# A two-layer block on one Trainium2 core: mean correlation with q and k exchanged, bias columns loaded by DMA, and the order of small work in the front and of the third batch changed

## The chip, the cores and the metric

The kernel runs on one core of a Trainium2 chip. The metric is device time in microseconds (us) of one execution. Five engines run in parallel, each in the order of its own instruction stream: TensorE (PE; its weight loads are shown apart as PEld), VectorE (DVE), ScalarE (ACT), GpSimd (POOL) and SyncE (SP). SP, ACT and POOL also issue DMAs, each into a queue of its own.

## What is computed

The input is x, 8 batches of 256 tokens of 256 features, and a context ctx of the same shape. Four residual steps follow each other, each on the layer norm of x:

```python
x = x + L0_xattn(layernorm(x), ctx, ctx, Wq, bq, Wout, bout)
x = x + L0_ffn(layernorm(x), centroids, ln_g, ln_b, w1, b1, w2, b2)
x = x + L1_xattn(layernorm(x), ctx, Wq, bq, Wkv, bkv, Wp, bp)
x = x + L1_ffn(layernorm(x), gate_W, w1_e, w3_e, w2_e, w1_s, w3_s, w2_s)

# L0_xattn: q, k, v have 16 features; corr is over the 256 positions
q, k, v = [(t @ Wq + bq).transpose(0, 2, 1) for t in (Q, K, V)]
corr = real(ifft(fft(q) * conj(fft(k)))).mean(axis=(0, 1))
W, I = top_k(corr, 12); W = softmax(W)
R = sum(w * roll(v, -shift) for w, shift in zip(W, I))
return tile_over_16_heads(R).reshape(8, 256, 256) @ Wout + bout

# L0_ffn: balanced assignment. Expert e takes the 256 tokens with the
# highest score for its centroid among those not yet taken, in turn.
h = layernorm(routed) ; h = gelu(h @ w1[e] + b1[e]) @ w2[e] + b2[e]

# L1_xattn: ordinary attention of 16 heads of 16, keys and values from ctx
# L1_ffn: top 2 of 8 experts (silu(x w1) * (x w3)) w2, plus 8 shared ones
```

## The kernel before

The 2,048 tokens lie in 16 tiles of 128 partitions (X for x, C for ctx; XT and CT are their transposes). The tile framework's scheduler is off: every engine runs its instructions in the order of the program text, so a wait of one instruction holds all that stand behind it on that engine. The one thing taken out of line is a queue, `work`, of products in steps of about 0.43 us: first the products of the second layer's keys and values, later those of the first layer's experts. `fill(us)` takes steps from it until so much time is used, and stands wherever PE would wait for another engine.

The stages, with the lines that matter here:

- **Loads (L1306 to L1342).** x and ctx come in eight loads on SP, the weights and biases behind them; bq, WZ and the centroids on ACT's queue. Two bias rows (`bq1`, `brow`) lie on one partition and are turned into columns on PE by `column` (L1256, products with `one1`).
- **Constants (L1493 to L1533).** On POOL and DVE: ident, `flip` (ones on the anti-diagonal, L1512), `a16` (L1507), the clearing of VA (L1523), `bsel`.
- **First projections.** `turn` transposes x and ctx; `stats_x` with its `newton()` gives each token's factor of the layer norm; `project` (L1447) makes q and k in one PSUM tile (`pqk`), batches stacked over the partitions. The factors, expanded (`rexp`, L1589) and transposed (`pR`, L1614), scale q; the bias is added to k (L1625).
- **Correlation (L1680 to L1777).** `pg` is the 256x256 product of k with q. Written to DRAM twice side by side (`Gd`) and read back with rows one element longer, its diagonals become columns (`DG`), and a product with a constant averages them: `pcorr`. While DG is on its way, PE transposes k (`vT`), multiplies Wout by flip (`woutr`, L1719; `wrt`, L1740), transposes boutb (`bt`), makes the first score product (`psx`) and takes `fill(1.73)`.
- **Shifts (L1780 to L1949).** The top 12 are found on DVE, their softmax weights written to DRAM (`Wd`) and read back skewed as a circulant (`CW`). `pr3` is CW times vT, `R3` its scaled copy, `pp` the product with woutr, `PB` that with boutb added. Meanwhile PE makes `ps0`, the row groups (`copy_rows`, two products of 128x512 each that put X into PSUM, where PB is added later), and small products for the scores (`pw`, L1887). `stay_warm` (L1929) puts a product that nobody reads behind pr3 and pp.
- **Scores and search.** X is completed, its scores for the centroids are made, and from L2202 a threshold search on DVE and PE finds each expert's tokens in turn, while PE runs the experts already found and the queue's products. `attention_columns` (L1369) is a generator of small preparations for the second attention, moved on by `next(columns)` at fixed places.
- **Second attention (L2960 to L3075).** A loop over batches and two halves of heads. Each turn makes `scores` (PE, L2687), exponentials (ACT, L2695) and the `values` of the turn before (PE, L2702). Batch b + 2 is prepared meanwhile: `add_y` adds the expert layer's rows (loaded two batches ahead by `load_y`), `batch_stats` makes mean and factor on DVE and POOL, `norm_q` normalises on DVE (L2616), `turn_q` transposes (L2640), `queries` projects (L2654); `add_bias` adds a bias to X on POOL (L2632). For the third batch (number 2) these lines stand in the turns of batch 0.
- **Second experts.** From here to the end PE runs the shared and the routed experts.

Of the kernel before, what the change touches and what calls it, by code (L numbers as in the profile page):

```python
# [9 lines left out]
F32 = mybir.dt.float32  # L10
# [4 lines left out]
ALU = mybir.AluOpType  # L15
# [1071 lines left out]
def fast_path(  # L1087
# [87 lines left out]
    one1 = const.tile([1, 1], F32, name="one1")  # L1175
    nc.vector.memset(one1, 1.0)
# [79 lines left out]
    def column(pool, tag, row, n):  # L1256

        pcol = pool.tile([P, n], F32, tag=tag, name="pcol")
        for j in range(n):
            nc.tensor.matmul(  # L1260
                pcol[:, j : j + 1],
                row[:, j * P : (j + 1) * P],
                one1,
                start=True,
                stop=True,
            )
        return pcol

# [26 lines left out]
    bq1 = pa.tile([1, DH], F32, name="bq1")  # L1295
    wout = pa.tile([P, KC, D], F32, name="wout")
    boutb = pa.tile([P, D], F32, name="boutb")
# [5 lines left out]
    brow = pst.tile([1, 2, H, DH], F32, name="brow")  # L1303
# [16 lines left out]
    nc.scalar.dma_start(out=bq1, in_=L0_xattn_bq.unsqueeze(0))  # L1320
# [6 lines left out]
    nc.scalar.dma_start(out=cen[:, 2, :], in_=L0_ffn_ln_b.partition_broadcast(E))  # L1327
    for src, dst in (
        (L0_xattn_Wout.rearrange("(lc p) n -> p lc n", p=P), wout),
        (L1_xattn_bq.unsqueeze(0), brow[:, 0].rearrange("o h d -> o (h d)")),  # L1330
        (bkv[:, 0, :].unsqueeze(0), brow[:, 1]),
        (L1_xattn_Wkv.rearrange("(kc p) n -> p kc n", p=P), wkv_in),
        (L1_xattn_Wq.rearrange("(kc p) n -> p kc n", p=P), wq),
        (L0_xattn_bout.partition_broadcast(P), boutb),
        (L0_ffn_ln_g.rearrange("(kc p) -> p kc", p=P), gbc[:, 0, :]),
        (L0_ffn_ln_b.rearrange("(kc p) -> p kc", p=P), gbc[:, 1, :]),
        (L0_ffn_b1.rearrange("e (fc p) -> (e fc) p", p=P), b1r),
    ):
        nc.sync.dma_start(out=dst, in_=src)
# [21 lines left out]
    bcol = pk.tile([P, 2, NB], F32, name="bcol")  # L1361
# [7 lines left out]
    def attention_columns():  # L1369


        pc = column(ps_k, "pm", brow.rearrange("o a h d -> o (a h d)"), 2 * NB)
        yield
        nc.vector.tensor_copy(bcol.rearrange("p a c -> p (a c)"), pc)
# [10 lines left out]
        pn = ps_k.tile([P, NB], F32, tag="pm", name="pn")  # L1385
        for c in range(NB):
            for kc in range(KC):
# [6 lines left out]
                )  # L1394
        nc.scalar.activation(qmax, pn, AF.Copy, scale=257.0)
# [51 lines left out]
    def project(which, weights, src):  # L1447

        for m in range(2):
            for kc in range(KC):  # L1450
                for g in range(4):
# [8 lines left out]
                    )  # L1460

# [9 lines left out]
    def rstd(mvs, r1, scale, eps, eng, mr=None):  # L1471
# [31 lines left out]
    a8 = pa.tile([P, 8], F32, name="a8")  # L1503
    nc.vector.tensor_reduce(
        a8, ident.rearrange("p (a i) -> p a i", i=16), AX.X, ALU.add
    )
    a16 = pa.tile([P, NCT, 16], F32, name="a16")  # L1507
    nc.vector.memset(a16, 0.0)
    for r in range(NCT):
        nc.vector.tensor_copy(a16[:, r, 8 * r : 8 * r + 8], a8)  # L1510

    flip = pa.tile([P, P], F32, name="flip")  # L1512
    nc.gpsimd.memset(flip, 1.0)
    nc.gpsimd.affine_select(
        out=flip,
        in_=flip,
        pattern=[[1, P]],
        compare_op=ALU.is_equal,
        fill=0.0,
        base=1 - P,  # L1520
        channel_multiplier=1,
    )
    nc.gpsimd.memset(VA[:, :, :, DH:], 0.0)  # L1523
    nc.gpsimd.memset(VA[:, :, :, DH : DH + 1], 1.0)
    bq8 = pa.tile([1, B, DH], F32, name="bq8")
    nc.gpsimd.tensor_copy(bq8, bq1.unsqueeze(1).to_broadcast([1, B, DH]))
# [9 lines left out]
    bqc = pa.tile([P, 1], F32, name="bqc")  # L1536
# [47 lines left out]
    newton = stats_x(12, nc.gpsimd)  # L1584
    turn(X, XT, 12, act, act)
    newton()

# [7 lines left out]
    turn(C, CT, 8, act, dve)  # L1595
    project(0, WC, XT)
    turn(C, CT, 12, act, dve)
    pc = column(ps_k, "pm", bq8.rearrange("o b c -> o (b c)"), 1)
    nc.vector.tensor_copy(bqc, pc)

# [10 lines left out]
    project(1, WZ, CT)  # L1611
# [11 lines left out]
    columns = attention_columns()  # L1623
    next(columns)
    nc.vector.tensor_scalar(qk[:, 1, :], pqk[:, 1, :], bqc, None, ALU.add)  # L1625
# [49 lines left out]
    )  # L1675
    cc.close()

# [6 lines left out]
    for tt in range(2):  # L1684
        nc.tensor.matmul(
            pgs[tt],
            qk[:, 1, tt * P : (tt + 1) * P],
            qk[:, 0, :],
            start=True,
            stop=True,  # L1690
        )
# [4 lines left out]
    for r in range(2):  # L1696
# [10 lines left out]
        in_=Gd[0, :].rearrange("(tt p w) -> p tt w", p=P, w=W2 + 1)[:, :, 0:S],  # L1707
    )

# [6 lines left out]

    pw = ps_t.tile([P, KC, D], F32, tag="pt", name="pw")
    for lc in range(KC):
        nc.tensor.matmul(  # L1719
            pw[:, lc, :], flip, wout[:, KC - 1 - lc, :], start=True, stop=True  # L1720
        )
    woutr = pa.tile([P, KC, D], F32, name="woutr")
    nc.scalar.copy(woutr, pw)
# [7 lines left out]
    for kc in range(KC):  # L1731
        pc = ps_t.tile([P, E], F32, tag="pt", name="pc")
        nc.tensor.transpose(pc, cg[:, kc * P : (kc + 1) * P], ident[:E, :E])
        nc.vector.tensor_copy(cenP[:, kc, 0:E], pc)
# [3 lines left out]
    for dc in range(KC):  # L1738
        for lc in range(KC):
            nc.tensor.matmul(  # L1740
                pw[:, dc, lc * P : (lc + 1) * P],
                wout[:, KC - 1 - lc, dc * P : (dc + 1) * P],
                flip,
                start=True,
                stop=True,
# [1744 lines left out]
```

## Time and profile before

| what | us |
|---|---|
| runs: lowest, median, highest of 3 | 883.21, 883.58, 884.36 |
| profiled execution, its own time | 878.96 |
| its span (first to last instruction) | 877.3 |
| PE busy in the span | 857.4 |
| DVE, ACT, POOL busy | 309.2, 265.6, 211.1 |
| mean granted PE clock | 0.997 of full |

The profile is of one execution, whose time is a little under those of the runs; differences within it are read against its own span. A matmul's row gives its start and its modelled duration; rows of one kind that follow each other are joined, with their number behind an x. In square brackets stands how long the engine had been idle before the row and what ended that.

### The profile page before, as it was taken

The numbers are of one execution on the slowest core, as the hardware profiler recorded it, in microseconds if no ns is written. First come the engines' busy times: TensorE is split into PE (matmuls) and PEld (weight loads), VectorE is DVE, ScalarE is ACT, GpSimd is POOL, SyncE is SP. The second block draws the span as 40 slices with busy tenths as digits, with TensorE's granted clock in tenths as the row PEclk, the third lists the DMA queues.
The fourth block names the chain that finished last, engine by engine and source line by source line (L and its number), as shares of the span: only waits on it lengthen the run. The fifth ranks groups of instructions, "written<-read, shape, count | busy, mean of one in ns | idle before, by whom it ended". The sixth has DMA issues, their size and how long they took to land. (4 is left out here: it accounts for less than half of the span.)

```text
span 877.3 us, 11190 instructions
## 1 busy us (share of the span) xinstructions
PE 857.4 (98%) x4204; PEld 535.2 (61%) x4204; DVE 309.2 (35%) x1028; ACT 265.6 (30%) x495; POOL 211.1 (24%) x292
## 2 busy tenths in 40 slices
PE   8899999999799999999999999999999999999997
PEld 7547788788355555545668474747464656474746
DVE  7388876502556665561111112021111111111011
ACT  4255543423677675321110111111111111111110
POOL 7061213311236364423310020111111121111200
PEclk9999999999999999999999999999999999999999
DMA  7485469731600001361110645564646434311130
GB/s 250 161 222 174 142 212 302 251 120 55 168 13 26 1 20 38 112 238 44 68 50 30 188 131 159 160 176 156 181 151 178 155 93 113 86 13 12 15 107 27
DMA packets 86282, 105.21 MB, mean 120 GB/s; under 512 B 7979, under 2 KB 76812, under 8 KB 86188
## 3 DMA queue, kind: packets, MB, share of 16 engines
q1 hardware_dynamic: 77706, 91.10, 32.6%
q0 software_dynamic: 7920, 13.02, 7.0%
q8 instruction: 35, 0.57, 0.3%
q10 hardware_dynamic: 594, 0.30, 0.1%
q14 instruction: 27, 0.22, 0.1%
HBM read 80.60 MB, written 25.37 MB: 121 GB/s over the span
## 5 line engine op out<-in xcount | busy, mean ns | idle before, releaser
L3119 DVE TENSOR_TENSOR A<-A,pu 128x512 f32<-128x512 f32 x96 | 66.0, 687 | 365.1 <-PE pu L3110 358.4
L3118 ACT ACTIVATE A<-pgt 128x512 f32<-128x512 f32 x96 | 57.4, 598 | 271.4 <-PE pgt L3110 271.3
L3179 POOL DMA_INDIRECT Od<-Y,ids x32 | 49.4, 1545 | 307.1 <-ACT Y L3192 215.0
L3110 PE MATMUL pgt<-RT,wa 128*128 128x512 f32 x256 | 121.1, 595 | 0.0
L3110 PE MATMUL pu<-RT,wb 128*128 128x512 f32 x256 | 120.3, 592 | 0.0
L3132 PE MATMUL py<-wc,A 128*128 128x256 f32 x512 | 111.8, 379 | 0.0
L3132 PEld LDWEIGHTS py<-wc,A 128*128 128x128 f32 x512 | 96.7, 190 | 13.3 <-issue 0.5
L2695 ACT ACTIVATE ex<-p,scale 128x512 f32<-128x512 f32 x128 | 77.2, 690 | 31.9 <-PE p L2687 30.7
L3110 PEld LDWEIGHTS pu<-RT,wb 128*128 128x128 f32 x256 | 48.6, 190 | 61.2 <-issue 60.0
L3110 PEld LDWEIGHTS pgt<-RT,wa 128*128 128x128 f32 x256 | 47.6, 190 | 54.9 <-issue 54.5
L2408 PE MATMUL ph<-RT,w 128*128 128x256 f32 x256 | 61.4, 389 | 0.2 <-ACT A L2417 0.2
L2425 PE MATMUL py<-w,A 128*128 128x256 f32 x256 | 61.3, 388 | 0.0
L2425 PEld LDWEIGHTS py<-w,A 128*128 128x128 f32 x256 | 46.6, 190 | 6.5
L2408 PEld LDWEIGHTS ph<-RT,w 128*128 128x128 f32 x256 | 45.3, 190 | 8.4 <-ACT A L2417 1.1
L2417 ACT ACTIVATE A<-ph,b1c 128x256 f32<-128x256 f32 x64 | 29.9, 472 | 58.4 <-PE ph L2408 56.5
L2927 POOL DMA_INDIRECT Td<-HP,to x32 | 31.6, 988 | 62.6 <-DMA Td<-HP,to 59.6
L3110 PE MATMUL pgt<-HT,wa_-1_2742 128*128 128x512 f32 x96 | 45.5, 596 | 0.0
L3110 PE MATMUL pu<-HT,wb_-1_2743 128*128 128x512 f32 x96 | 45.1, 592 | 0.0
L3192 ACT ACTIVATE Y<-py,R 128x256 f32<-128x256 f32 x32 | 15.1, 473 | 96.6 <-PE py L3132 93.5
L2687 PE MATMUL p<-QM,KT 32*128 32x512 f32 x256 | 42.9, 650 | 0.4 <-DVE QM L2668 0.4
L3132 PE MATMUL py<-wc_-1_2744,A 128*128 128x256 f32 x192 | 41.9, 379 | 0.0
L3132 PEld LDWEIGHTS py<-wc_-1_2744,A 128*128 128x128 f32 x192 | 36.4, 190 | 5.8 <-issue 1.0
(467 smaller groups left out, 991.6 us busy)
## 6 DMA issues: line engine op xcount, KB each, us to landing
w<-in_L_ffn_w_dram SPq DMA_DIRECT2D x16, 1024.0 KB
wa<-in_L_ffn_w_e_dram SPq DMA_DIRECT2D x8, 1024.0 KB
wb<-in_L_ffn_w_e_dram SPq DMA_DIRECT2D x8, 1024.0 KB
wc<-in_L_ffn_w_e_dram SPq DMA_DIRECT2D x8, 1024.0 KB
R<-Td SPq DMA_DIRECT2D x8, 530.0 KB
sa<-in_L_ffn_w_e_dram SPq DMA_DIRECT2D x16, 256.0 KB
sb<-in_L_ffn_w_e_dram SPq DMA_DIRECT2D x16, 256.0 KB
sc<-in_L_ffn_w_e_dram SPq DMA_DIRECT2D x16, 256.0 KB
```

The lines of the kernel that those rows point to most:

```text
L2408: nc.tensor.matmul(ph, w1[:, kc, f * P : (f + 1) * P], RT[:, kc, :], start=(kc == 0), stop=(kc == KC - 1),)
L2417: nc.scalar.activation(A[:, f, :], ph, AF.Gelu_apprx_tanh, bias=b1c[:, e, f : f + 1])
L2425: nc.tensor.matmul(py, A[:, f, r * P : (r + 1) * P], w2[:, f, :], start=(f == 0), stop=(f == NF - 1),)
L2687: nc.tensor.matmul(ps[g].rearrange("p m q -> p (m q)"), KT[rows, c, k0 : k0 + P], QM[b][rows, c].rearrange("p m q -> p (m q)"), start=True ...
L2695: nc.scalar.activation(e4[:, g], ps[g], AF.Exp, scale=scale)
L2927: nc.gpsimd.indirect_dma_start(out=Td, out_offset=bass.IndirectOffsetOnAxis(ap=to[g][:, k, j : j + 1], axis=0), in_=HP[:, GT * g + j, :], ...
L3110: nc.tensor.matmul(ps, w_[:, kc, fs], xs[kc], start=(kc == 0), stop=(kc == KC - 1),)
L3118: nc.scalar.activation(a, pgt, AF.Silu)
L3119: nc.vector.tensor_tensor(a, a, pu, ALU.mult)
L3132: nc.tensor.matmul(py, A[:, f, s : s + P], wc[:, f, :], start=(f == 0), stop=(f == NF - 1))
L3179: nc.gpsimd.indirect_dma_start(out=Od, out_offset=bass.IndirectOffsetOnAxis(ap=ids, axis=0), in_=Y, in_offset=None, compute_op=ALU.add,)
L3192: nc.scalar.activation(Y, py, AF.Copy, scale=R[:, i, D + e : D + e + 1])
```

## The change

- q and k change places in `pg`: the columns of the product are those of k. The diagonals run the other way, so DG is read from offset 1, CW with rows one element shorter, and vT's halves are taken in reverse. With that `flip`, `woutr` and the products with flip go; `wrt` is made by transposes, and `pp` uses Wout itself.
- The bias columns come by DMA: `bqc` through a copy of bq in DRAM (`bqd`, ACT's queue), `bcol` from L1_xattn_bq and through `bkd` (SP), `boc` from bout. `column`, `one1`, `bq1`, `bq8`, `brow` and `bt` go.
- `project` runs over kc outside and m inside and yields after each kc; `pR` stands between the halves of the second call. k's bias is added on ACT. The last `newton` is called with DVE.
- `rowsel` is made on POOL from a constant; the centroids' transposes stand before `pg`; b1's transpose and the parts of `attention_columns` stand elsewhere.
- `fill(1.73)` becomes `fill(4.3)`.
- After the top 12, three row groups instead of five stand before `pr3`; the other two stand where `stay_warm` stood.
- In the second attention `add_y(2)` and `batch_stats(2)` follow `norm_q(1)`, and `norm_q(2)` follows `turn_q(1)`.

```diff
-    nc.scalar.dma_start(out=bq1, in_=L0_xattn_bq.unsqueeze(0))
+    nc.scalar.dma_start(
+        out=bqd.rearrange("o (b c) -> (o b) c", b=B),
+        in_=L0_xattn_bq.partition_broadcast(B),
+    )
...
+    nc.scalar.dma_start(out=bqc, in_=bqd.rearrange("o (p x) -> p (o x)", x=1))
     for src, dst in (
+        (bkv[:, 0, :].unsqueeze(0), bkd.rearrange("o (h d) -> o h d", h=H)),
         (L0_xattn_Wout.rearrange("(lc p) n -> p lc n", p=P), wout),
-        (L1_xattn_bq.unsqueeze(0), brow[:, 0].rearrange("o h d -> o (h d)")),
-        (bkv[:, 0, :].unsqueeze(0), brow[:, 1]),
+        (L1_xattn_bq.rearrange("(c p) -> p c", p=P), bcol[:, 0, :]),
         (L1_xattn_Wkv.rearrange("(kc p) n -> p kc n", p=P), wkv_in),
         (L1_xattn_Wq.rearrange("(kc p) n -> p kc n", p=P), wq),
+        (bkd.rearrange("o (c p) -> p (o c)", p=P), bcol[:, 1, :]),
         (L0_xattn_bout.partition_broadcast(P), boutb),
+        (L0_xattn_bout.rearrange("(kc p) -> p kc", p=P), boc),
...
-        for m in range(2):
-            for kc in range(KC):
+        for kc in range(KC):
+            for m in range(2):
...
+            yield
...
-    newton = stats_x(12, nc.gpsimd)
+    newton_l = stats_x(12, nc.gpsimd)
     turn(X, XT, 12, act, act)
     newton()
+    turn(C, CT, 8, act, dve)
+    newton_l(nc.vector)
...
-    project(1, WZ, CT)
+    projected = project(1, WZ, CT)
+    next(projected)
     pR = ps_a.tile([P, S], F32, tag="pg", name="pR")
...
-    columns = attention_columns()
-    next(columns)
-    nc.vector.tensor_scalar(qk[:, 1, :], pqk[:, 1, :], bqc, None, ALU.add)
+    list(projected)
+    nc.scalar.activation(qk[:, 1, :], pqk[:, 1, :], AF.Identity, bias=bqc)
...
-            qk[:, 1, tt * P : (tt + 1) * P],
-            qk[:, 0, :],
+            qk[:, 0, tt * P : (tt + 1) * P],
+            qk[:, 1, :],
...
-        in_=Gd[0, :].rearrange("(tt p w) -> p tt w", p=P, w=W2 + 1)[:, :, 0:S],
+        in_=Gd[0, :].rearrange("(tt p w) -> p tt w", p=P, w=W2 + 1)[:, :, 1 : S + 1],
...
+    columns = attention_columns()
     next(columns)
-    fill(1.73)
+    pb1 = ps_t.tile([P, E * NF], F32, tag="pt", name="pb1")
+    nc.tensor.transpose(pb1, b1r, ident[: E * NF, : E * NF])
+    b1c = pr.tile([P, E, NF], F32, name="b1c")
+    nc.scalar.copy(b1c.rearrange("p e f -> p (e f)"), pb1)
+    fill(4.3)
...
-        in_=bass.AP(wd.tensor, wd.offset + 1, [[WD + 1, P], [P, 2], [1, S]]),
+        in_=bass.AP(wd.tensor, wd.offset + P - 1, [[WD - 1, P], [P, 2], [1, S]]),
...
-    for b in order_b[:3]:
-        copy_rows(b, ps_t, "pt")
...
-    pw = ps_a.tile([P, 4, 32], F32, tag="pg", name="pw")
+    pw = ps_t.tile([P, 4, 32], F32, tag="pt", name="pw")
...
-        if j == 0:
-            copy_rows(order_b[3], ps_t, "pt")
-        elif j == 1:
-            copy_rows(order_b[4], ps_k, "pm")
+    copy_rows(order_b[0], ps_t, "pt")
+    copy_rows(order_b[1], ps_t, "pt")
+    small_products(0)
+    small_products(1)
+    copy_rows(order_b[2], ps_t, "pt")
+    small_products(2)
...
-                vT[:, sc, :],
+                vT[:, 1 - sc, :],
...
-    stay_warm(pr3[:, 2:4, :].rearrange("p a q -> p (a q)"), 1)
+    copy_rows(order_b[3], ps_t, "pt")
...
-    stay_warm(pp2[:, 1, :], 1)
+    copy_rows(order_b[4], ps_k, "pm")
...
     norm_q(1, nc.vector, nc.vector)
+    add_y(2)
+    batch_stats(2, "q")
     add_bias(0)
...
                 turn_q(1)
+                norm_q(2, nc.vector, nc.vector)
                 queries(1, 0)
                 queries(1, 1)
-                add_y(2)
-                batch_stats(2, "q")
...
                 else:
-                    norm_q(2, nc.vector, nc.vector)
                     add_bias(2)
```

## The prediction

> **What bounds the kernel now.** I read the page's totals first, then a table of windows, then the order in time of the windows in which TensorE (PE) is not full.
>
> ```profile
> span 877.3 us, 11190 instructions
> ...
> PE 857.4 (98%) x4204; PEld 535.2 (61%) x4204; DVE 309.2 (35%) x1028; ACT 265.6 (30%) x495; POOL 211.1 (24%) x292
> ```
>
> PE is idle for 877.3 - 857.4 = 19.9 us in all. More than that can be gained only by taking PE work away or by clock. The table says where the idle time is (window, its length, PE's busy time first; the column after POOL is the granted clock):
>
> ```profile
> 0.00:20.00 20.00, 17.24 (x159) 14.29 (x160) 15.90 (x62) 8.61 (x15) 15.27 (x39) 1.00 0.84 274
> 20.00:31.00 11.00, 9.77 (x61) 6.78 (x62) 4.19 (x16) 3.14 (x7) 3.59 (x15) 1.00 0.23 73
> 40.00:57.00 17.00, 14.47 (x99) 6.80 (x98) 11.71 (x51) 7.38 (x20) 6.96 (x19) 1.00 1.09 325
> 79.00:100.00 21.00, 21.00 (x140) 16.22 (x139) 18.70 (x89) 11.27 (x25) 2.90 (x3) 1.00 0.35 119
> 230.00:240.00 10.00, 6.07 (x48) 3.12 (x52) 5.24 (x13) 3.88 (x8) 2.76 (x6) 0.98 1.08 291
> 240.00:260.00 20.00, 20.00 (x171) 10.20 (x165) 9.72 (x25) 14.54 (x25) 4.18 (x14) 0.92 0.05 15
> ```
>
> So there are three places: the front up to 57, bound by chains of dependent steps; the search beside the experts from 79, where PE is full and each product removed counts; and 230 to 240, with 3.93 us idle and a lower clock behind it. The front's rows (start, duration, engine, line, in brackets the wait):
>
> ```profile
> 19.06 0.49 POOL L1589 COPY rexp<-R 128x256 f32<-128x256 f32 x1
> ...
> 20.48 1.05 PE L1260 MATMUL pcol<-one,brow 1*128 1x1 f32 x8
> ...
> 21.47 1.13 PE L1685 MATMUL pg<-qk 128*128 128x256 f32 x4
> ...
> 30.28 1.13 PE L1777 MATMUL pcorr<-DG,mean_w 128*128 128x256 f32 x4 [1.03 <-DMA DG<-Gd]
> ...
> 39.80 1.13 PE L1933 MATMUL pr<-vT,CW 128*128 128x128 f32 x8 [0.47 <-PE pw L1898]
> ...
> 41.40 0.48 DVE L1942 TENSOR_SCALAR R<-pr,rtot 128x256 f32<-128x256 f32 x1 [0.66 <-PE pr L1929]
> ...
> 43.54 0.42 DVE L1949 TENSOR_TENSOR PB<-pp,boutb 128x256 f32<-128x256 f32 x1 [1.66 <-PE pp L1929]
> ```
>
> R3 and PB wait on L1929, the two dummy products, not on the products they read. The attention's rows:
>
> ```profile
> 224.51 1.23 DVE L2607 TENSOR_TENSOR b_t<-b_r,b_ve 128x2 f32<-128x2 f32 x1 [0.81 <-POOL b_r L2602]
> ...
> 237.99 0.78 PE L2640 MATMUL pt<-ident,h 128*128 128x128 f32 x4 [3.60 <-DVE h L2616]
> ...
> 239.81 1.94 PE L2702 MATMUL pv<-ex,VA 128*32 128x256 f32 x16
> 239.87 2.42 ACT L2695 ACTIVATE ex<-p,scale 128x512 f32<-128x512 f32 x4 [4.05 <-PE p L2687]
> ...
> 241.67 2.15 PE L2687 MATMUL p<-QM,KT 32*128 32x512 f32 x8
> ```
>
> PE waits 3.60 us for batch 2's normalised rows, and then the same products take twice as long (1.94 against 1.07 at 243.75; 2.15 against 1.17): a window of 3.4 us at half clock, 1.7 us lost.
>
> **Part 1, third batch sooner.** Before, add_y(2) starts on DVE at 233.41, POOL's Newton steps end at 237.40, norm_q(2) runs 237.43 to 238.16. Now add_y(2) and its statistics follow norm_q(1), which ends at 227.10, or 225.9 since the 1.23 us row loses its cover (POOL's bias add, 224.46 to 225.72, now comes later). Add 0.68 + 1.2 + 0.2: about 228.0. POOL takes 2.1 (235.34 to 237.40 before): 230.2. norm_q(2) follows turn_q(1)'s copy at 230.27 and ends near 231.0. PE needs it at 234.39, where pv of 233.32 ends, so the wait goes. What is late next is ACT: its exponentials run 2.42 per half, back to back from 233.41: 235.83, 238.25. Then the last pv of the pair starts near 238.5 and queries(2) near 239.6, against 244.75: **-5.1**. Bounds: -3.6 (the wait alone, the clock window falling elsewhere) and -5.6 (all idle 3.9 plus 1.7). Behind it the attention is PE-bound (20.00 of 20), so the gain stays. Moved with it: the VA copies at 227.02 come 1 to 1.5 later on DVE, before their readers; POOL's two bias adds run 230.3 to 232.9, read much later; load_y(4) stands on SP ahead of the weights issued from 226.74 and costs these under 1 us, hundreds before use; yg(2), issued from 214.5, is there.
>
> The row of 224.51 shows a DVE instruction that takes 1.23 instead of 0.16 (its twin at 215.53) until POOL's add ends. [...]
>
> **Part 2, front up to pcorr.** The flips (L1719 1.03, ACT 0.59), boutb's transposes (0.38) and brow's columns (1.05) leave PE; all but the last lay in the wait for DG. The first chain is rexp -> pR -> Rq -> qk -> pg. Chunk 8's Newton is still called twice on POOL (its name is rebound only for the last chunk), so rexp keeps its 19.06; VA's 3.50 us memset is now ahead of ident's select, which shifts the start of DVE's statistics by some 0.2. pR now stands between the halves of project(1): pR 19.75 to 20.45, second half 1.15 more, ACT's qk copy 0.5, so pg at 22.2 against 21.47: **+0.7** for pg, G and pcorr (31.0). Bounds 0 (rexp early enough) to +1.0 (ident's delay in full). In the wait for DG stand now 10 key products for 4 (fill 4.3 for 1.73): PE is ready at about 30.5, ahead of 31.0, so they are covered; were G early they would cost the difference.
>
> Bias columns: on SP one load of 1 KB to DRAM and three of 4-byte pieces replace brow's two. The trace's two loads of that kind (gbc) issue at 13.57 and 15.08, b1r at 15.85; at 1.5 each b1r moves to about 18, landing near 21. First readers now: bqm and pb1, ahead of the keys, about 26. Gd's issue stands behind them on SP, at 23.75. Covered by 5 us: 0. On ACT's queue a wait for bqd stands ahead of the table load (2.94); the first copy is at 5.98, the load and warm end 1.5 after start: 0, bound +0.5.
>
> **Part 3, pcorr to the search.** Before: pr3 starts 9.5 after pcorr since PE does five row groups (1.12 each) and pw's bank must be read first. Now only three groups and pw in another bank come before it, so PE is free 7.0 after pcorr, and pr3 waits for CW, whose last packets come 8.2 after pcorr (38.48), with 0.25 to its release: 8.45. That is -1.05. Without L1929 R3 and PB start at their products' ends: 41.40 -> 40.95 and 43.54 -> 43.1, in all -0.83; the two row groups fill the holes instead. With +0.7: -1.15 at the search (56.93). It meets a second bound: the first expert's rows go through DMA queues that the 40:57 row shows full (325 GB/s), and what is issued behind CW comes 0.25 earlier at most. I take **-0.9** for front and start, bounds -1.9 and +0.7. The small moves at 55.95 to 57.5 (pn, b1c, rowsel) sit beside DVE's chain: 0.
>
> **Part 4, products moved out of the full stretch.** Six products of two matmuls, 0.216 from start to start (95.75: six in 1.46), are 2.6 us. In the orders of both kernels two to three of the six are missing where the queue of work has run empty, near 97 to 102 and 156.5, and there PE waits for DVE's or POOL's result anyway (0.44 at 156.56). So three to four count: **-1.4**, bounds 0 and -2.6.
>
> **Sum**: -5.1 - 0.9 - 1.4 = -7.4. The profiled run took 878.96 (span 877.3): 871.6. The runs' median is 883.58, 4.62 above it; by the same difference the forecast is **876.2**. The ends of all terms give -2.9 and -10.1: 880.7 and 873.5.
>
> **Rivals.**
> - Everything counts (all six products, the front uncapped): -10.1, 873.5. For: PE is at 21.00 of 21. Against: the empty queue and the full DMA. 0.15.
> - The front nets a loss and the products move nothing: -5.1 + 0.7 = -4.4, 879.2. For: pg's +0.7 is sure, the gains behind it hang on CW's landing, and DVE is 18.70 of 21 busy beside the search, so PE's gain may turn into a wait for the count. Against: 0.47, 0.66 and 1.66 are waits whose releaser is removed. 0.17.
> - The third batch's gain is lost to another wait (rows held on DVE or POOL past 234.39 by the whole 3.6): -2.3, 881.3. Against: 3.4 us of room. 0.06, half of it within 0.2%.
> - Slower: the chain of small loads on SP. bkd's landing holds SP, then boutb, boc, gbc, b1r and Gd stand behind. Free while its last issue is before 23.75; then 1 us per us; slower than before by over 0.2% from 23.75 + 7.4 + 1.8 = 33, that is if its four added loads take 4 us each instead of 1.5. At 5 each: 887. For: no row has a DRAM round trip there while the loads of x and ctx fill the queues (274 GB/s). Against: the 1.5. 0.08.
>
> **How the numbers follow.** Forecast 0.54; its own range -5.6 to -9: 874.6 to 878. What a measurement can tell from no change is 0.2%, 1.8 us. Faster: 0.54 + 0.15 + 0.17 + 0.03 = 0.87 less 0.02 for a front loss on top; same 0.06, slower 0.09. The range takes in the bounds: 873.0 to 881.0.
>
> **What would show it.** Right: pg near 22.2, pcorr near 31.0, pr3 near 39.5, the search's first count near 55.8, no 3.60 before turn_q's third transpose, clock 1.00 from 240 to 260. Wrong: SP issuing Gd after 24; pcorr behind the key products; a wait of PE for h; idle PE between 79 and 213 equal to the removed products.

## The result, and the profile after

The changed kernel takes 879.94 us (median of 13 runs, 878.52 to 882.78) beside 883.93 for the kernel before in the same runs (13, 881.84 to 886.74): a ratio of 0.9957, with a 95% interval from 0.9946 to 0.9969. That is 4.0 us less, of 7.4 forecast; 879.94 lies inside the range of 873 to 881. The sign was right, and only about half the size came; that the time lies in the range is owed to the range's width, not to the sum.

The profiled executions differ far less, 878.58 against 878.96: that of before was 5.0 us under its own median, that of after 1.4. So sizes are taken from the timed runs here, and the traces are read for where the time goes. The page's totals after:

```profile
span 876.9 us, 11139 instructions
...
PE 854.9 (98%) x4178; PEld 533.2 (61%) x4178; DVE 306.5 (35%) x1022; ACT 266.1 (30%) x494; POOL 213.3 (24%) x293
```

PE is busy 2.5 us less, but its idle time grew from 19.9 to 22.0. The table of windows (after the window its length, then the busy time of PE, PEld, DVE, ACT and POOL, the granted clock, the share of the DMA queues and GB/s) says where:

```profile
0.00:20.00 20.00, 16.45 (x127) 14.48 (x130) 12.34 (x55) 8.48 (x15) 13.77 (x34) 0.91 0.91 269
20.00:31.00 11.00, 10.16 (x80) 6.39 (x78) 3.97 (x17) 4.27 (x11) 6.46 (x20) 1.00 0.29 80
40.00:57.00 17.00, 15.88 (x100) 7.36 (x100) 11.55 (x50) 7.47 (x21) 6.79 (x19) 1.00 1.07 336
57.00:79.00 22.00, 19.27 (x105) 13.60 (x105) 16.82 (x77) 7.61 (x18) 8.85 (x15) 1.00 0.65 172
79.00:100.00 21.00, 20.14 (x136) 15.38 (x135) 18.78 (x89) 11.59 (x25) 2.90 (x3) 1.00 0.37 132
100.00:213.00 113.00, 109.52 (x614) 89.56 (x615) 53.92 (x229) 45.21 (x96) 26.24 (x26) 1.00 0.63 190
230.00:240.00 10.00, 9.22 (x72) 4.62 (x72) 7.00 (x14) 6.71 (x12) 5.26 (x8) 1.00 0.96 253
240.00:260.00 20.00, 20.00 (x176) 10.59 (x176) 10.01 (x25) 14.93 (x26) 4.97 (x16) 1.00 0.19 59
```

And two of the windows before:

```profile
57.00:79.00 22.00, 21.43 (x117) 15.14 (x117) 17.77 (x82) 10.01 (x25) 8.62 (x15) 1.00 0.59 162
100.00:213.00 113.00, 112.38 (x632) 92.79 (x631) 53.16 (x225) 44.87 (x96) 26.83 (x27) 1.00 0.62 191
```

From 40 to 57 and from 230 to 240 PE is fuller than before (15.88 for 14.47, 9.22 for 6.07), and behind 240 the clock is whole. But from 57 to 79 PE is 2.16 us less busy, and in the long stretch from 79 on, where PE had been full, there are now holes (20.14 for 21.00, and 109.52 for 112.38). The span cut at two fixed marks, the first count of the search on DVE and `pbp`, the small product that ends the first experts' stretch on PE:

| profiled execution | start to first count | first count to pbp | pbp to end |
|---|---|---|---|
| before | 56.93 | 155.85 | 664.5 |
| after | 57.11 | 158.86 | 660.9 |
| forecast of the difference | -0.9 | -1.4 | -5.1 |
| measured in these two | +0.2 | +3.0 | -3.6 |

So the third batch delivered, the front gave nothing, and the stretch from which products were taken became longer. These are single executions: the kernel before's own front and stretch, in the traces of `e1_third_only` and `e14_third_again` below, give 56.03 and 56.31 to the first count and 157.54 and 156.65 from there to `pbp`; the changed kernel's two repeats give 57.22 and 57.11, and 157.88 and 158.85. Over all of them the stretch is longer by 1.9 rather than 3.0. In the front the rows after are (start, duration, engine, line; in brackets the wait):

```profile
20.06 0.40 POOL L1561 COPY rexp<-R 128x256 f32<-128x256 f32 x1
...
23.93 1.13 PE L1674 MATMUL pg<-qk 128*128 128x256 f32 x4 [0.84 <-DVE qk L1596]
...
27.70 4.58 PE L1398 MATMUL pp<-CT,WK 128*128 128x256 f32 x20
...
32.12 1.03 PE L1751 MATMUL pcorr<-DG,mean_w 128*128 128x256 f32 x4
...
40.28 1.16 PE L1906 MATMUL pr<-vT,CW 128*128 128x128 f32 x8 [0.94 <-DMA CW<-Wd]
...
41.47 0.48 DVE L1915 TENSOR_SCALAR R<-pr,rtot 128x256 f32<-128x256 f32 x1 [0.71 <-PE pr L1906]
...
43.20 0.42 DVE L1921 TENSOR_TENSOR PB<-pp,boutb 128x256 f32<-128x256 f32 x1 [1.24 <-PE pp L1918]
```

`pg` comes 2.46 later than before, not 0.7. The clock of 0.91 in the first window is not why: in `e3_fill_short`, where the clock of that window is 1.00, `pg` comes at 23.96. `pcorr` has no wait in brackets: it stands directly behind 20 key matmuls of 4.58 us, on PE and not on DG. From `pcorr` to `PB` it takes 11.08 instead of 13.26. PE's waits between 57 and 213, before:

```profile
PE prt L2391 <- ACT R L2371: 0.4, 1, 0.4
PE pid L2308 <- DVE ob L2304: 0.2, 1, 0.2
```

and after (us in total, times, longest):

```profile
PE prt L2355 <- ACT R L2335: 2.6, 4, 1.2
PE pcn L2183 <- DVE above L2166: 2.5, 2, 1.4
PE pid L2272 <- DVE ob L2268: 1.1, 2, 0.9
PE ph L2372 <- ACT RT L2359: 0.7, 1, 0.7
```

The reader sees four kinds of waits that were nearly hidden before: PE comes to a result of the search (`pcn`, `pid`), to an expert's rows (`prt`) or to their transposes (`ph`), and has nothing left in its queue of work to do first. The two waits for `pcn` lie between 57 and 79.

The attention's rows after:

```profile
227.70 0.16 DVE L2571 TENSOR_TENSOR b_t<-b_r,b_ve 128x2 f32<-128x2 f32 x1 [0.81 <-POOL b_r L2566]
...
233.08 2.55 POOL L2596 TENSOR_TENSOR X<-X,bpb 128x512 f32<-128x512 f32 x2
233.38 2.40 DVE L2580 TENSOR_SCALAR h<-X,b_mv,b_r 128x256 f32<-128x256 f32 x2
...
237.52 0.66 PE L2604 MATMUL pt<-ident,h 128*128 128x128 f32 x4
...
240.13 1.07 PE L2666 MATMUL pv<-ex,VA 128*32 128x256 f32 x16
...
243.79 1.99 PE L2618 MATMUL pp<-hT,wq 128*128 128x256 f32 x8
```

The wait of 3.60 is gone (237.52 has none), and pv takes 1.07, not 1.94. `norm_q(2)` is held beside POOL's two bias adds, 2.40 us instead of 0.73, but is ready 1.74 before PE asks.

### The profile page after: what moved, and what is told of

Its sections match the earlier page's. It is cut to its first block, busy times and chain, and to the rows that moved or that the text cites. A ratio compares the mean times of both kernels' runs of the same rounds, so it can differ in the third digit from the quotient of the medians.

```text
span 876.9 us, 11139 instructions
## 1 busy us (share of the span) xinstructions
PE 854.9 (98%) x4178; PEld 533.2 (61%) x4178; DVE 306.5 (35%) x1022; ACT 266.1 (30%) x494; POOL 213.3 (24%) x293
## 4 chain that ended last, share of the span: by engine, by line
PE 87%; DMA 5%; DVE 3%; POOL 2%; ACT 1%; issue 1%; SPq 0%; POOLq 0%; DVEq 0%; ACTq 0%
PE pgt L3074 19%; PE py L3096 19%; PE pu L3074 19%; PE py L2389 5%; PE ph L2372 4%; PE p L2651 4%; PE pv L2666 3%; DMA R<-NMd,ids 3%; PE pp L2717 2%; PE pp L2618 2%; PE pp L1419 2%; PE pp L1398 1%; PE pgu L3269 1%; PE pt L3130 1%; PE pt L1512 1%
```

## The experiments

The kernel before was timed beside every group, so each ratio is against it. In the traces "four", "six" or "ten" products are the key products that `fill` takes while DG is on its way: `fill(1.73)`, `fill(2.5)` and `fill(4.3)`.

### The third batch alone

`e1_third_only`, the kernel before with this edit:

```diff
     norm_q(1, nc.vector, nc.vector)
+    add_y(2)
+    batch_stats(2, "q")
...
+                norm_q(2, nc.vector, nc.vector)
...
-                add_y(2)
-                batch_stats(2, "q")
...
-                    norm_q(2, nc.vector, nc.vector)
```

> The kernel before with the third batch's move alone. Theory 1 (the move is nearly all of the change's gain, and the rest of the change nets about nothing): the same gain as the trace of after shows inside the attention, 4.1 us (queries(2) 0.97 earlier although the attention began 3.19 later), so a ratio near 0.9954, like that of the whole change (0.9957). Rival (the rest of the change is worth 1 us or more of its own): 3 us or less here, ratio 0.9966 or above. In the trace either way: no wait of some 3.6 before the third batch's transposes, clock 1.00 from 240 to 260.

Measured: 876.75 beside 881.76, ratio 0.9941 (0.9925 to 0.9958), 5.2 us less. It is faster than the whole change. Its window of 230 to 240:

```profile
230.00:240.00 10.00, 9.22 (x72) 4.59 (x69) 5.21 (x7) 7.10 (x13) 4.33 (x6) 1.00 1.11 303
```

PE 9.22 as in the whole change, clock whole. So the part carries all of the gain alone, and the rest of the change together loses. It was run once more beside other kernels:

> The third batch's move alone once more: 0.9925 to 0.9955, at or under the changed kernel of this group.

875.92, ratio 0.9948 (0.9928 to 0.9967): 4.6 us less. The time holds.

### The bias columns' round trip

`e2_bias_on_sp`, the changed kernel with both loads of `bqd` moved from ACT's queue to SP's list behind x and ctx:

```diff
-    nc.scalar.dma_start(
-        out=bqd.rearrange("o (b c) -> (o b) c", b=B),
-        in_=L0_xattn_bq.partition_broadcast(B),
-    )
...
-    nc.scalar.dma_start(out=bqc, in_=bqd.rearrange("o (p x) -> p (o x)", x=1))
...
+        (L0_xattn_bq.partition_broadcast(B), bqd.rearrange("o (b c) -> (o b) c", b=B)),
...
+        (bqd.rearrange("o (p x) -> p (o x)", x=1), bqc),
```

> The changed kernel with bq's round trip through DRAM taken from ACT's queue and put into SP's list behind the loads of x and ctx. Theory 2 (this round trip is what made the front late: ACT's table load waits for it, 5.46 instead of 2.94, and the loads of x and ctx behind the second one are issued later): third and later x loads at 4.9 to 5.3 as before, first copy of XT near 6.2, pg at 22.2 to 22.7 instead of 23.93, and with it the rows for the second search land in time; time 1.5 to 3 us under the changed kernel, ratio 0.992 to 0.994. Rival (the front is late for another reason, such as ident's later select or DVE): pg stays at 23.5 or later, ratio 0.995 to 0.997.

Measured: 875.52, ratio 0.9929 (0.9912 to 0.9947). ACT's rows in the changed kernel:

```profile
0.81 1.28 ACTq L1309 DMA_DIRECT2D bqd<-in_L_xattn_bq_dram  x1
...
5.01 0.42 ACTq L1320 DMA_DIRECT2D bqc<-bqd  x1
5.46 1.28 ACT L1336 ACT_TABLE_LOAD   x1 [5.46 <-DVE B L1344]
```

and SP's:

```profile
1.32 0.49 SPq L1307 DMA_DIRECT2D C<-in_ctx_dram  x1
5.00 0.37 SPq L1307 DMA_DIRECT2D X<-in_x_dram  x1
```

With the round trip on SP, in `e2_bias_on_sp`, SP's third load:

```profile
1.85 0.51 SPq L1307 DMA_DIRECT2D X<-in_x_dram  x1
```

and ACT's table load there:

```profile
3.16 1.28 ACT L1333 ACT_TABLE_LOAD   x1 [3.16 <-issue]
```

In the changed kernel two engines stand still until 5.00: ACT, whose `bqc` waits for `bqd`, and SP, whose third load is not issued. SP's list has no data from ACT; yet what its queue waits for in the changed kernel (us in total, times, longest) is

```profile
SPq L1307 <- DMA bqd<-in_L_xattn_bq_dram: 3.2, 1, 3.2
```

Its third load waits until ACT's first DMA has landed, at 4.99. Why it waits for that DMA was not shown. `pg` comes at 22.66 and the first count at 55.60 when this is gone, against 23.93 and 57.11.

`e6_bqc_late` undoes half of it; `bqc` is issued from ACT behind the table load:

```diff
-    nc.scalar.dma_start(out=bqc, in_=bqd.rearrange("o (p x) -> p (o x)", x=1))
...
+    nc.scalar.dma_start(out=bqc, in_=bqd.rearrange("o (p x) -> p (o x)", x=1))
```

> The changed kernel with the load of bqc behind the table load in ACT's program: the round trip still goes through ACT's queue, but the table load no longer waits for it. Theory 2a (the table load's wait is what made the front late): table load near 3.7, first copy of XT at 6.0 to 6.3, pg near 22.7 as with the round trip on SP's queue; ratio 0.9925 to 0.994. [...]

880.12, ratio 0.9947 (0.9928 to 0.9965). The table load starts at 3.79 and SP's third load at 1.85, but now its fourth, C, is held until 4.89, 2.7 us of that by the landing of WZ, the next DMA on ACT's queue. `pg` comes at 23.04, so the front is 0.9 sooner, and the time is that of the whole change. Theory 2a is not met whole: the stall moves on by one load, and what the front gains does not reach the end while ten products are taken.

### The ten products

`e3_fill_short`, the changed kernel with one number:

```diff
-    fill(4.3)
+    fill(1.73)
```

> The changed kernel with fill(1.73) instead of fill(4.3): four key products in the wait for DG instead of ten. Theory 3 (the six products held pcorr up, since DG's last packets came at 31.0 and PE was busy until 32.1, and further back they leave holes instead of time): pcorr near 31.2, PE's waits at pid near 99 and at prt near 159 and 176 shrink by 2 us or more, time 0.5 to 2 us under the changed kernel, ratio 0.9935 to 0.995. Rival (my prediction: PE is the bound from 79 to 213 and the six products are worth 1.4 us): 1 us or more slower than the changed kernel, ratio 0.997 or above.

876.83, ratio 0.9939 (0.9921 to 0.9956). With four products PE does wait for DG, and this is how long:

```profile
31.22 1.10 PE L1751 MATMUL pcorr<-DG,mean_w 128*128 128x256 f32 x4 [1.50 <-DMA DG<-Gd]
```

1.50 us was to be covered, not the 2.6 that six more products take; `pcorr` is 0.9 earlier than with ten, and there are no holes near 97 to 101. The interval of the ratio overlaps that of the change, so the time alone does not tell four from ten here.

`e9_third_fill` is the other direction: the kernel before, with the third batch's move and `fill(4.3)`, and nothing else of the front.

> The kernel before with the third batch's move and fill(4.3) alone, so against the move alone (0.9941) it shows the six products by themselves. Theory 3 (they are paid in the front, where only 1.0 us of PE's wait for DG was free, and come back as holes): pcorr some 1.3 later than with the move alone, waits of about 0.86 at pid and 0.66 at ph near 97 to 100 that the move alone did not have, sometimes a window at half clock behind them; ratio 0.9955 to 0.9975. Rival (the six products are worth time in the full stretch): ratio 0.993 or lower.

879.13 beside 880.84, ratio 0.9986 (0.9974 to 0.9998): the ten products alone take back some 3.7 us of the third batch's gain (0.9941 and 0.9948 without them). `pcorr` in `e1_third_only`:

```profile
29.47 1.03 PE L1777 MATMUL pcorr<-DG,mean_w 128*128 128x256 f32 x4
```

and PE's rows in `e9_third_fill`:

```profile
32.03 1.03 PE L1777 MATMUL pcorr<-DG,mean_w 128*128 128x256 f32 x4
...
99.71 0.55 PE L2308 MATMUL pid<-ob,oab 128*16 128x16 f16 x16 [0.86 <-DVE ob L2304]
...
101.51 0.70 PE L2408 MATMUL ph<-RT,w 128*128 128x256 f32 x2 [0.65 <-ACT RT L2395]
102.07 1.88 PE L2408 MATMUL ph<-RT,w 128*128 128x256 f32 x4
```

The cost is paid three times over. `pcorr` is 2.56 later, since G is early here and PE is still busy with key products. Two holes, 0.86 and 0.65, open where the missing products would have stood. And the last row shows what follows: the clock falls to half for 3.4 us from 102.3, and four matmuls take 1.88, those from 104.03 on 1.93. In the changed kernel's first trace, where the clock stays whole, the same four:

```profile
101.77 1.11 PE L2372 MATMUL ph<-RT,w 128*128 128x256 f32 x4
```

`e7_sp_fill` joins both repairs, the bias loads on SP and `fill(1.73)`:

> The changed kernel with the round trip on SP's list and fill(1.73), both. If theories 2 and 3 are right and their costs lie in different places (front; pcorr and the search), they add: pg near 22.6, pcorr near 29.9, no holes at 97 to 99, no half clock there, ratio 0.990 to 0.992. Rival (both act on the same slack, the rows' DMA stream or the search's chain on DVE): no better than the better one of them, 0.9925 or above.

878.59, ratio 0.9935 (0.9916 to 0.9953). The two do not add. The first count comes at 54.88, 2.2 before that of the change, and 14.54 later the second search stands still for its row of scores:

```profile
69.42 0.75 DVE L2155 SCALAR_TENSOR_TENSOR n<-n,lo,row 128x512 f32<-128x512 f32 x1 [1.73 <-DMA row<-SCd]
```

By its place it would be the bound by DMA that the forecast named, a step further on: `row` is issued on SP's queue (at 65.02 in the trace of after), as the experts' weights are (from 37.90). It does not bind in every execution, though. The same step waits 1.53, 1.20 and 0.23 in three traces of the changed kernel (the first, `e5_after_again`, `e13_after_third`), and 0.23 in `e2_bias_on_sp` and `e18_sp_fill_six`, which have the front and the loads of `e7_sp_fill`.

### The front without the third batch

`e10_front_alone` is the change with `fill(1.73)` and the third batch where it was before.

> The changed kernel without the third batch's move and with fill(1.73): what is left is the front. Theory (its gain of 2 us between pcorr and the search is paid back by the late pg and stopped by the rows of the second search): ratio 0.9985 to 1.0005. Rival (my prediction's -0.9 for the front, or more): 0.9985 or lower.

881.45, ratio 1.0006 (0.999 to 1.0022). The front's rearrangement by itself is worth nothing that can be measured, and its first count, 56.29, lies among those of the old front with four products (56.93, 56.03, 56.31). Its attention has the old gap, with two stretches of 3.413 us at half clock from 238.0.

### Repeats of the change

`e5_after_again` and `e13_after_third` are the changed kernel, unaltered, in other groups.

> The changed kernel itself, unchanged, as the reference of this group of runs. Expected: a ratio of 0.9946 to 0.9969 as first measured. The trace is read for what differs from execution to execution: the wait of 1.53 for the second search's row, which the other kernel with the same front did not have, and the windows at half clock (one at 12 to 15 us first; behind the holes near 99 in the other).

> The changed kernel once more, as reference of this group: 0.993 to 0.9965; the waits at pid (0.86) and ph (0.66) near 97 to 101 are there again.

879.51, ratio 0.9947 (0.993 to 0.9965), and 877.61, ratio 0.9961 (0.9946 to 0.9977). With the first result the mean of the three ratios is 0.9955. The same holes are in all three traces (0.85 or 0.86 for `pid`, 0.66 for `ph`); the half clock behind them is in that of `e13_after_third`, but not in the other two. Its windows:

```profile
79.00:97.00 18.00, 18.00 (x112) 13.79 (x111) 16.08 (x77) 10.30 (x23) 2.91 (x3) 1.00 0.41 143
97.00:104.00 7.00, 5.49 (x35) 3.75 (x34) 4.61 (x20) 2.06 (x5) 0.98 (x1) 0.76 0.63 209
104.00:120.00 16.00, 16.00 (x99) 12.95 (x98) 11.93 (x55) 7.75 (x17) 3.92 (x4) 1.00 0.53 144
```

PE is full before and behind; between, 1.51 us idle and a clock of 0.76: 3.413 us at half.

### Other orders in the front

`e8_front_order`: on top of `e7_sp_fill`, q's product ahead of k's addition, a short memset ahead of the long one on POOL, Newton's steps of chunk 8 once.

```diff
+    pad = pa.tile([P, P], F32, name="pad")
+    nc.gpsimd.memset(pad, 0.0)
     nc.gpsimd.memset(VA[:, :, :, DH:], 0.0)
...
-    newton()
...
-    nc.scalar.activation(qk[:, 1, :], pqk[:, 1, :], AF.Identity, bias=bqc)
     nc.vector.tensor_tensor(qk[:, 0, :], pqk[:, 0, :], Rq, ALU.mult)
+    nc.scalar.activation(qk[:, 1, :], pqk[:, 1, :], AF.Identity, bias=bqc)
```

> As the kernel with both, and further: the product that scales q stands ahead of the bias addition to k in the text (the trace of after shows DVE waiting for ACT's write to the other half of the same tile, 2.74 us of idle), a small memset ahead of VA's so that ident's select comes before VA's 3.5 us, and the Newton steps of the third chunk run once. Theory: DVE's start returns to near 5.3 and pg comes 0.4 to 0.9 sooner than with the two alone (near 21.9); time 0.3 to 1 us under it, ratio 0.989 to 0.991. Rival (the loads of x and ctx bound the front): pg unchanged within 0.2, ratio equal.

878.62, ratio 0.9941 (0.992 to 0.9962). DVE's statistics start at 4.92 instead of 5.84 in the change, but `pg` is at 22.88 against 22.36 in `e7_sp_fill`: no gain.

`e11_w1_late`: on top of `e7_sp_fill`, the second expert's weights are loaded behind the rows.

```diff
-    W0 = {e: load_l0(e) for e in range(2)}
+    W0 = {0: load_l0(0)}
...
+    W0[1] = load_l0(1)
```

> As the kernel with the round trip on SP's list and fill(1.73), and the second expert's weights (2 MB) loaded behind the rows of the search and not ahead of them. Theory 5 (the front's gain ends at the rows: in the kernel with both the search begins at 54.88, 2.05 sooner than before, but the second search's first step only 0.71 sooner, 69.42, since its row is behind a full DMA stream): that step comes 13.2 after the search's start, near 68.1, and time is 1.3 us under the kernel with both, ratio 0.9915 to 0.9925. Rival (the row is late for another reason, such as the small pieces of the means written from 56 on): the step stays at 69 or later, ratio as with both, 0.9935.

875.54, ratio 0.9941 (0.9924 to 0.9958). The wait for the row falls:

```profile
68.43 0.75 DVE L2156 SCALAR_TENSOR_TENSOR n<-n,lo,row 128x512 f32<-128x512 f32 x1 [0.20 <-DMA row<-SCd]
```

13.01 after the first count instead of 14.54, and none of the four traces with the weights late (`e11_w1_late`, `e12_split_qk`, `e15_split_qk_again`, `e16_fill_six`) has more than 0.21 there. That fits the weights in the queue as the cause, but does not show it, since `e2_bias_on_sp` and `e18_sp_fill_six` have the weights ahead and wait 0.23. Nor does the time: 0.9941 against 0.9935, within both intervals.

`e12_split_qk`: on top of `e11_w1_late`, q and k in two tiles, with the short memset and the single Newton call of `e8_front_order`.

```diff
-    qk = pa.tile([P, 2, S], F32, name="qk")
+    q_s = pa.tile([P, S], F32, name="q_s")
+    k_s = pa.tile([P, S], F32, name="k_s")
...
-    nc.scalar.activation(qk[:, 1, :], pqk[:, 1, :], AF.Identity, bias=bqc)
+    nc.scalar.activation(k_s, pqk[:, 1, :], AF.Identity, bias=bqc)
-    nc.vector.tensor_tensor(qk[:, 0, :], pqk[:, 0, :], Rq, ALU.mult)
+    nc.vector.tensor_tensor(q_s, pqk[:, 0, :], Rq, ALU.mult)
```

> As the kernel with the second expert's weights late, and q and k in two tiles, so that DVE's product does not wait for ACT's addition, a small memset ahead of VA's, Newton steps once. Theory: the product starts within 0.6 of the end of Rq's copy or of the projection, pg 0.4 to 0.5 sooner against the start of pR than in the kernel with both (there 2.76 behind pR's start), DVE's first statistics at 4.9; with the rows no longer in the way this shows in the time: 0.4 to 1 us under the kernel with the weights late. Rival (rows or DMA still bound): no difference.

> The kernel with the round trip on SP's list, fill(1.73), the weights late and q and k in two tiles. Theory (its attention began 1.1 sooner than with the move alone, and what follows is bound by PE): 0.7 to 1.5 us under the move alone. Rival (the time goes back in the waits for gathered rows between 150 and 180): equal within 0.5.

874.8, ratio 0.9935 (0.9923 to 0.9948), and, run again, 875.72, ratio 0.994 (0.9922 to 0.9959). DVE's product still starts at 21.87, only after ACT's addition of 21.37 and 0.47, and `pg` follows `pR` by 2.76 as in `e7_sp_fill`: the two tiles did nothing, and the second run is at the rival's figure. What holds DVE there was not found: `Rq` is written by 20.71 and the outputs are apart, but both still read the one PSUM tile `pqk`.

### Six products

The runs so far say that four leave 1.50 us of PE's wait open and ten overfill it. Two more, at 0.43 each, fill 0.87 of it, and six in all leave 0.63. `e16_fill_six` is `e12_split_qk` with that, `e17_after_fill_six` the change itself, `e18_sp_fill_six` is `e2_bias_on_sp`:

```diff
-    fill(4.3)
+    fill(2.5)
```

> As e15 with fill(2.5): six products in the wait for DG for four. Theory (holes): pcorr is not later, PE's wait for DG 0.65 instead of 1.51, but the queue is two products shorter: waits at pid or ph near 95 to 100, or longer ones at prt from 150 on, by 0.5 to 0.9 in all; time equal to e15 or up to 0.8 slower. Rival (only pcorr's delay made fill(4.3) lose): 0.9 us under e15.

> The changed kernel with fill(2.5), one edit: six products in the wait for DG, which the trace of the run with four showed to be 1.50 long. If the number decides: pcorr near 31.2 as with four, ratio 0.990 to 0.993, and the waits at prt from 150 on under 1 in all. If the place decides: ratio 0.9935 to 0.9955, waits at prt from 150 on of 1.5 or more.

> The changed kernel with the round trip on SP's list and fill(2.5). If the number decides: 0.989 to 0.992, waits at prt from 150 on under 1 in all. If the place decides: 0.992 to 0.995.

| products | ratios to before (95%) | first count to pbp in the traces |
|---|---|---|
| ten | change 0.9957 (0.9946-0.9969), 0.9947 (0.993-0.9965), 0.9961 (0.9946-0.9977); bias on SP 0.9929 (0.9912-0.9947) | 157.9 to 161.6 in seven executions |
| four | change 0.9939 (0.9921-0.9956); bias on SP 0.9935 (0.9916-0.9953); two tiles 0.9935 (0.9923-0.9948), 0.994 (0.9922-0.9959) | 155.9 to 160.5 in ten |
| six | change 0.992 (0.9904-0.9937); bias on SP 0.9913 (0.9894-0.9931); two tiles 0.991 (0.9895-0.9925) | 155.3 to 155.6 in three |

Six are best in each of the three fronts tried; on the changed kernel itself, where one number is the only edit, the intervals of six and ten do not touch. Four against ten is less clear: with the bias on SP four gain nothing. The three with six take 872.57, 873.98 and 873.22, 3 to 4 us less than the change by the ratios. `e16_fill_six` is 3.1 under its twin with four, `e15_split_qk_again`, more than the 0.9 that covering the wait would give, so that neither of its two theories is met; it is the fastest of all that were timed. Six in the old front with the third batch's move were not run, so what the new front adds to the six is not known. PE's rows in `e17_after_fill_six`, one number away from the change:

```profile
27.68 2.86 PE L1398 MATMUL pp<-CT,WK 128*128 128x256 f32 x12
...
31.17 1.10 PE L1751 MATMUL pcorr<-DG,mean_w 128*128 128x256 f32 x4 [0.63 <-DMA DG<-Gd]
...
172.16 0.60 PE L2355 MATMUL prt<-ident,R 128*128 128x128 f32 x4
```

and its waits from 57 to 213:

```profile
PE pcn L2183 <- DVE above L2166: 1.1, 1, 1.1
PE ph L2372 <- ACT RT L2359: 0.7, 1, 0.7
PE prt L2355 <- ACT R L2335: 0.4, 2, 0.3
```

`prt` waits 0.4 in all, where the change waits 2.6, its longest at

```profile
176.32 0.44 PE L2355 MATMUL prt<-ident,R 128*128 128x128 f32 x2 [1.23 <-ACT R L2335]
```

Part of the reason may be the order of the queue's products: with another number taken early, other products stand at every later fill. Why it is just with six that the last experts' rows come in time, where four still leave a wait of 1.23 near 174 in `e1_third_only`, is open: POOL's gathers of those rows start 1.9 earlier (164.86 against 166.75 in `e3_fill_short`), but the traces do not say how much of that is cause and how much is effect.

### The hold on DVE beside POOL

`e4_bias_adds_late`: the bias adds of batches 0 and 1 moved behind `norm_q(2)`.

```diff
-    add_bias(0)
-    add_bias(1)
...
                 norm_q(2, nc.vector, nc.vector)
+                add_bias(0)
+                add_bias(1)
```

> The changed kernel with POOL's two bias adds behind norm_q(2) in the text. Theory 4 (norm_q(2) took 2.40 instead of 0.73 because POOL's adds of 2.55 ran beside it, and that costs nothing, since PE asks for the rows 1.7 later): norm_q(2) 0.73, the rows ready 1.7 sooner, turn_q(2) and queries(2) at the same distance from the attention's start as in the changed kernel (16.2 and 22.5 from queries(0)'s second half), no gain. Rival (the missing 1 us of the attention's gain is this hold): queries(2) 0.8 to 1.0 nearer to the start.

878.88 in one run. `norm_q(2)` again takes 2.40 beside POOL's 2.55: POOL had nothing else to do and started at once, so the order in the text did not part the two. The distance from queries(0) to queries(2) is 22.38 for 22.39. Inconclusive on what the hold costs where it isn't covered; here it is covered.

## Why the prediction was half right

The term that was missed most is that of the six key products: taken as covered in the wait for DG and as worth 1.4 us behind it, they cost time in both places. The second is the bias round trip, priced at 0.

**Part 1, the third batch (-5.1): right**, in its mechanism and nearly in its size. Alone it gave -5.2 and -4.6. In the trace the way from queries(0) to queries(2) went from 26.54 to 22.39, -4.15; `queries(2)` was 1.0 later than forecast, because ACT's exponentials are not back to back but have gaps of 0.24 and 0.60 for their scores. The rest fits the clock. A stretch of 3.413 us at half clock costs half its length, 1.7 us, or 0.0019 of the mean clock over 880 us; the runs of the third batch alone had a mean clock of 0.9990 and 0.9988, those of before in the same two groups 0.9962. That is 2.3 to 2.5 us of clock, of which the profiled execution shows, within its 4.15, only the one stretch, of 1.7, that the forecast counted; no run takes the clock by itself. The 1.23 on DVE became 0.16 when POOL's add moved, as forecast. `norm_q(2)` took 2.40 beside POOL's 2.55, where before it took 0.73, and its room was enough: it was ready 1.74 before PE asked.

**Part 2, pg +0.7: it came 2.46 later, and the step that failed is the bias round trip, priced at 0 with a bound of 0.5.** I looked at what ACT does behind its wait (the table load and the first copy), and priced ACT. I did not look at what the DMA of another queue may hold: SP's third load, 1.86 before, went at 5.00. Without the round trip on ACT, `pg` was at 22.66, 22.36 and 22.37 (`e2_bias_on_sp`, `e7_sp_fill`, `e18_sp_fill_six`); the old front has it at 21.47, 21.85, 22.14 and 21.82 in four traces (before, `e1_third_only`, `e14_third_again`, `e9_third_fill`). By the means that is +0.6, so the +0.7 for the rest of the front was sound, and the round trip, at 23.93 in the change, put some 1.5 on top. Its price at the end depends on the rest: 0.9955 to 0.9929 with ten products, 0.9920 to 0.9913 with six, where the intervals overlap.

**Part 2, the ten key products "covered": failed.** I had PE ready at 30.5 ahead of DG at 31.0, with a margin of 0.5 taken from the one DG read in the trace of before (issued at 26.00, last packets at 29.7). After, DG was issued at 28.43 and its packets ended at 30.8, 2.3 and not 3.7 later. With four products PE waits 1.50; ten took 2.6 more and held `pcorr`.

**Part 3, pcorr to the search (-1.88 before the cap): the way from `pcorr` to `PB` went down by 2.18**, with `pr3` on CW and the dummy products' waits gone, as forecast. But the late `pg` and the products ahead of `pcorr` eat it (count +0.2), and where they are removed (`e7_sp_fill`) the second search waited for its row in that trace. By itself the front, with the round trip on ACT, gave 1.0006.

**Part 4, six products moved out of the full stretch (-1.4): wrong in sign.** The step that failed is "there PE waits for DVE's or POOL's result anyway", used as a cover for two or three of the six. It is no cover, it is the cost: a product that fills a wait is worth its whole time, and taken away it leaves a hole (0.86, 0.66) and behind it, at times, half a clock. Two of the signs that I had named for being wrong came: `pcorr` behind the key products, and idle PE between 79 and 213, 3.7 us more of it for 2.6 of products removed. From four to ten the change lost 1.4 us by the ratios (0.9939 to 0.9955, with overlapping intervals), the kernel before with the third batch 3.7. From four to six it gained 1.7 (0.9939 to 0.9920, overlapping too); the two that moved fill a wait that was truly empty, 0.87 of it, and the rest is open. With ten made six the change is at 0.9920, by that 7.0 us under before: this one number holds nearly all that was missing of the 7.4. That it then comes so near is luck, for the forecast counted on ten.

Summed by the runs: -4.9 for the third batch (mean of two), +0.5 for the front with four products (`e10_front_alone`, its interval from -0.9 to 1.9) and +1.4 for the ten: -3.0, where -4.0 was measured. Beside the third batch the front with four gives -0.5 rather than +0.5 (0.9939 against 0.9945), which makes up the difference; both lie in one interval. The nearest rival was the one in which the front nets a loss and the products move nothing, 879.2. The slower one, SP's chain of small loads, did not come: Gd's issue, at 25.50, is behind the 24 that I had named as a sign, but it followed G at once, and G was late.

## What to carry to other kernels

Fill in a wait is worth as much as the wait is long, so measure the wait with the filler at its smallest, and take no more than fits: 1.50 us held two more products of 0.43 and not six more, and those that did not fit delayed `pcorr` and left holes in the place they were taken from. Before a load is made into a round trip on one queue, look at which other queue is held by it, as SP's was here for 3.2 us. When the profiled execution lies 5 us under its own median, look at the clock of the timed runs before taking a sum from it.

## What the runs showed of the hardware

**Half clock after short holes.** A stretch at half clock lasts 3.413 us in the traces of before (from 239.69) and after (from 11.74), and a clock of 0.76 over the 7 us from 97, as `e13_after_third`, `e2_bias_on_sp` and `e4_bias_adds_late` have it, is that of one such stretch; `e10_front_alone` has twice that. In `e13_after_third` two holes of 0.85 and 0.66 us, 1.5 us idle in two pieces, lie between 97.0 and 100.4, and the clock falls at 100.4. In the changed kernel's first trace the holes come 1.3 later (98.55 to 99.41 and 100.54 to 101.20), and the clock stays whole, 1.00 from 79 to 213. The other traces with these two holes are divided as well: in `e2_bias_on_sp`, `e4_bias_adds_late` and `e9_third_fill` the clock falls, near 98.3, 99.2 and 102.3 by the clock of their windows; in `e5_after_again` and `e6_bqc_late` it is 1.00 from 79 to 120. What decides between the two was not shown. This is read from seven traces and not tried by itself. Nor did 1.5 us idle bring it everywhere: in `e7_sp_fill` PE is idle for 1.63 us ahead of 71.02, and the six matmuls behind take 1.54, as the six at 55.74 do.

**A DMA of ACT held a load of SP**, issued at 1.86 before and at 5.00 in the change, 3.2 us of it in a wait for that DMA's landing at 4.99, without data between them.

**The read of DG from DRAM** took 2.3 us in the trace of after and 3.7 in that of before, from issue to its last packets, for the same bytes; with the old front it took 2.3, 2.3 and 3.2 in three more (`e1_third_only`, `e14_third_again`, `e9_third_fill`), so the execution decides and not the change.
